# Chained copies and later transposes in layer 1, row sums ahead of widened reciprocals in layer 0, small loads by GpSimd at the head

## The chip, the core and the metric

The kernel runs on one core of a Trainium2 chip. A core has five engines that work side by side, each with its own in-order queue of instructions: TensorE (PE in the profile) multiplies matrices and writes the results to PSUM; VectorE (DVE) and ScalarE (ACT) compute on SBUF and PSUM; GpSimd (POOL) computes on SBUF; SyncE (SP) issues DMA transfers, which ACT and POOL can issue as well. Engines wait for each other by semaphores. The metric is the time of one execution on the device in microseconds, the median of several runs.

## What is computed

Eight images of 32 x 32 positions (1024 tokens) and 384 channels go through two layers. Layer 0 normalises by groups of channels and applies attention of six heads with 64 channels each, with learned tables of relative positions. Layer 1 applies causal attention of one head with 384 channels, and a feed-forward part with weights reduced to signs.

```python
# layer 0: attention over an image
qkv = gn(x) @ qkv_w + qkv_b                     # q, k, v of six heads
attn = (q * HD ** -0.5) @ k.T + rel_h + rel_w   # 1024 x 1024 for each head
x = x + softmax(attn) @ v @ proj_w + proj_b
# layer 1: attention over the same tokens, then the feed-forward part
q, k, v = (ln(t) @ w for w in (Wq, Wk, Wv))
t = t + softmax(causal(q @ k.T * C ** -0.5)) @ v
h = gelu(bitlinear(ln(t), W1, b1))
t = t + bitlinear(h, W2, b2)
```

The part `bitlinear` uses the signs of the weights' differences from group means and quantises its result by the largest absolute value of an image. Images 5, 6 and 7 get no feed-forward result.

## The kernel before

The images run one after the other in the order 5, 0, 1, 2, 3, 4, 6, 7 (`ORDER`), so "the first image" is image 5. The kernel is written in a framework that orders the instructions of each engine by priorities and a model of their times, allots buffers and sets all semaphores. The source steers this order with `tc.issue_after(ins)`: instructions inside such a block that run on the same engine as `ins` are placed behind it in that engine's queue. It adds no wait between engines. `behind_of` is the same, and does nothing when given none. PSUM has one pool of eight tiles of 128 x 512 (`o_tile`), one bank each; a tile is given out again once its readers are done.

**The head (`run`, L1366 on).** `load_factors` loads the two factors of layer 1's combined query-key weight by SP and ACT. `load_T` loads the first image transposed, in six pieces of 256 KB, three by SP and three by ACT. `load_weights` then issues the small loads by ACT: two for the rows of biases (L148, L149), four for the position table `rel` (L151, L152), whose rows are 252 bytes long; SP loads the weights (`wproj_sb`, three thirds of `qkv_w`, and two biases spread over the partitions). A square root on a constant (`early_root`) makes ACT load its table. PE multiplies the factors out (`multiply_out`, nine steps, f_wqk), in between forms the group means and variances (two small matmuls, f_gmean and f_gvar), turns the bias rows (`turn_biases`, L169) and adds the value bias times the projection to the projection bias (`join_biases`, L376, f_pb). ACT scales `rel` (L171) and copies and scales the biases (L170, L172, L173). DVE takes the statistics (L434), finishes the normalisation (L451, three slices of 1024 columns) and forms `fold` (L235), a small matrix of ones by which PE can add row sums. The first projection of queries (`project_qk`, f_qk at L558) needs the normalised image. POOL builds sums of weights (`weight_forms`). A matmul of fp32 data appears in the profile as two records.

**Product sets (`ProductSet`).** A product of 3 x 3 blocks of weights with 3 x 2 blocks of input is done with 15 multiplications in place of 18 (`PROD_ORDER`). Sums of inputs (`sum_forms`, L568) and of weights are made beforehand. Each product goes to one of six banks A to F; `keep` copies partial sums from a bank with ACT (L623), and `run` combines some copies (L643; on POOL in layer 1). When a bank has all its products and its partner is ready, `finish` calls `final`, which on DVE adds bank and copy into the result: `put_queries` (L1069) or `put_values` (L1077) in layer 1. `in_turn` gives all these matmuls one fixed order on PE.

**Layer 0's attention (`attend0_fast`).** Three pairs of heads times two halves of the queries, six stretches. In each, PE computes scores (L889, L893) for eight key tiles, ACT takes exponentials (L900), DVE adds the eight tiles up (`add_up`, L905, L907), and PE multiplies with the values (L915, f_av). The row sums follow: DVE transposes the total in 32 x 32 blocks (L924) and reduces it (`few`, L926). In five stretches `gathered` brings `few` into its layout by five DMAs and DVE adds (L952); in the last stretch PE adds by `fold` (L947, f_den). `reciprocals` takes the reciprocals (L954), records two checks (L545, L546), widens them by a copy (L958) and a block transposition (L959), and a multiplication scales the result oT. It is done one stretch later: for the fifth stretch (third pair, half 0) within the last one, and multiplied by DVE (L977); for the last stretch at once (L987). Then PE projects the result, eight tiles f_pj in three steps each (L504); the third step of tiles 0 to 3 reads what L977 wrote.

**Layer 1's head (`attention1`, L1086 on).** The projected tiles are added to the image (`more`, L995), normalised by rows in two halves of four tiles (`normed`: L461, L462, L465, ACT's root L467, the reciprocal L469 and four scalings L474, f_xn), and turned by PE (`turn_normed`, L414, f_pt, copied by ACT at L415). Half 0's query products run (`of_q`, f_pr_1q), in whose course half 1 is normalised and turned, followed by half 0's value products (`of_v`, f_pr_1v) and half 1's.

Of the kernel before, what the change touches and what calls it, by code (L numbers as in the profile page):

```python
# [11 lines left out]
F32 = mybir.dt.float32  # L12
# [79 lines left out]
def conv_attn_hybrid(  # L92
# [51 lines left out]
    def load_weights(pools):  # L144

        nc.vector.memset(rel, 0.0)
        rows = pools.page("rows")[: 3 * NC + NM, :P]
        nc.scalar.dma_start(out=rows[: 3 * NC, :], in_=qkv_b.rearrange("(m p) -> m p", p=P))  # L148
        nc.scalar.dma_start(out=rows[3 * NC :, :], in_=b1.rearrange("(m p) -> m p", p=P))  # L149
        for half in range(2):  # L150
            nc.scalar.dma_start(out=rel[half * HD : (half + 1) * HD, 0, : 2 * H - 1], in_=rel_hT)  # L151
            nc.scalar.dma_start(out=rel[half * HD : (half + 1) * HD, 1, : 2 * W - 1], in_=rel_wT)  # L152
# [8 lines left out]
        nc.sync.dma_start(out=b2_sb, in_=b2.partition_broadcast(P))  # L161

        early = pools.small.tile([P, 1], F32, tag="early", name="early_root")
        first_root[0] = nc.scalar.activation(early, ones[:, 0:1], AF.Sqrt).ins
        return raw, rows

    def turn_biases(pools, rows):
        ps = pools.o_tile("biases")
        nc.tensor.transpose(ps[:, : 3 * NC + NM], rows, ident[: 3 * NC + NM, : 3 * NC + NM])  # L169
        nc.scalar.copy(biases, ps[:, : 3 * NC + NM])  # L170
        nc.scalar.mul(rel, rel, 1.0 / qscale)  # L171
        nc.scalar.mul(bqk[:, 0:NPAIR], bqk[:, 0:NPAIR], qscale)  # L172
        nc.scalar.mul(bqk_neg, bqk, -1.0)  # L173
# [199 lines left out]
    def join_biases(pools):  # L373
        ps = pools.o_tile("pb")
        for k in range(NC):
            nc.tensor.matmul(  # L376
                ps[:, :C], bv[:, k : k + 1].to_broadcast([P, P]), wproj_sb[:, k, :], start=(k == 0), stop=(k == NC - 1)
            )
# [3 lines left out]
    def load_factors(pools):  # L382
# [4 lines left out]
        return wqT_sb, wkT_sb  # L387

# [16 lines left out]
    def stages(pools):  # L405

        last_transpose, last_mean, last_root, last_normed = [None], [None], [None], [None]

# [18 lines left out]
        def group_norm_T(b, xT=None):  # L427

            xT = load_T(b) if xT is None else xT
# [20 lines left out]
            for k in range(NC):  # L450
                nc.vector.tensor_scalar(  # L451
                    xT[:, k, :], xT[:, k, :], cs[:, 0:1], cs[:, 1:2], ALU.subtract, ALU.mult
                )
# [138 lines left out]
        class ProductSet:  # L592

            def __init__(self, name, forms, weights, width=512, tiles=None, bias=False, eng=None):
# [4 lines left out]
                self.full, self.behind = [], None  # L599
# [18 lines left out]
            def keep(self, ps, name):  # L618
                dst = self.kept(name)
                end = next((end for end in PROD_ENDS.values() if end[0] == name), None)  # L620
                with behind_of(self.behind):
# [251 lines left out]
        def attend0_fast(residual, b, q, k, r, v, later):  # L873
# [5 lines left out]
            last_exp, last_matmul = [None], [None]  # L879
# [41 lines left out]
            def over_tiles(p, half, total):  # L921
# [4 lines left out]
                nc.vector.tensor_reduce(few, tr.rearrange("p (a n i) -> p a n i", a=2, i=32), AX.X, ALU.add)  # L926
# [567 lines left out]
```

## Time and profile before

| | us |
|---|---|
| runs shown: lowest, median, highest of 3 | 2284.01, 2284.54, 2287.18 |
| the profiled execution | 2285.15 |
| its span, first to last instruction | 2283.4 |
| busy: ACT | 1208.8 (53%) |
| busy: POOL | 523.9 (23%) |
| chain that ended last: share of PE, DVE, DMA | 91%, 5%, 1% |
| granted TensorE clock | 0.998 |

An engine's busy time is the sum of its instructions. The waits list who stood idle, what ended it, the total, how often, and the longest. In a timeline each line has a start, a duration, the engine, the line of the source, the operation, the tile written and the tiles read, and how many instructions are merged; in brackets stands the idle time just before and what ended it. PE's ends are modelled and matmuls overlap in the pipeline, so that distances between starts say more than durations there. One image takes some 307 us; the first one's layer 0 projection starts at 164.89, the third one's at 710.48.

### The profile page before, as it was taken

The page shows a single profiled execution, that of the slowest core. Times are in us where ns is not written, and L with a number is a line of the kernel's source. Part 1 is how long each engine was busy: PE and PEld are TensorE (multiplying, and loading weights), DVE is VectorE, ACT ScalarE, POOL GpSimd, SP SyncE. Part 2 cuts the span into 40 slices and gives each one's busy share as a digit, 9 for nine tenths or more (in the row PEclk, how much of TensorE's full clock was granted, in tenths as well). Part 3 has the DMA queues.
Part 4 walks back from the last instruction along what each step waited for, and adds up shares of the span by engine and source line. Part 5 has one row for each costly group of instructions (what it writes and reads, how often), then busy time and mean ns, then how long its engine had stood idle before and what let it go on. Part 6 is the DMA issues. An engine that isn't in the chain of part 4 may idle for free.

```text
span 2283.4 us, 30117 instructions
## 1 busy us (share of the span) xinstructions
PE 2254.1 (99%) x10579; PEld 1382.8 (61%) x10579; DVE 1635.1 (72%) x2743; ACT 1208.8 (53%) x2181; POOL 523.9 (23%) x690
## 2 busy tenths in 40 slices
PE   8999999999999999999999999999999999999998
PEld 4547554768645677547685465874577754755474
DVE  6898578876888548886468884579854788737871
ACT  4654266337664457644467543766444766326641
POOL 6512222230141301313102313013040131221320
PEclk9999999999999999999999999999999999999999
DMA  7530562140730205520319203064002362017100
GB/s 182 155 92 28 157 140 59 39 165 29 150 103 29 73 39 125 127 58 1 111 43 184 55 29 111 28 147 106 30 20 92 96 147 68 1 52 160 43 1 30
DMA packets 182938, 188.54 MB, mean 83 GB/s; under 512 B 139717, under 2 KB 152378, under 8 KB 179962
## 3 DMA queue, kind: packets, MB, share of 16 engines
q1 hardware_dynamic: 164400, 115.85, 21.0%
q0 software_dynamic: 17184, 69.22, 9.7%
q8 instruction: 86, 1.41, 0.3%
q10 hardware_dynamic: 1194, 1.45, 0.2%
q14 instruction: 74, 0.61, 0.1%
HBM read 84.55 MB, written 51.58 MB: 60 GB/s over the span
## 4 chain that ended last, share of the span: by engine, by line
PE 91%; DVE 5%; DMA 1%; issue 1%; ACT 1%; ACTq 0%; DVEq 0%; SPq 0%
PE f_s L889 12%; PE f_av L915 12%; PE f_s L1157 8%; PE f_av L1172 8%; PE f_y L1332 7%; PE f_y L1282 7%; PE f_pj L504 5%; PE f_qk L558 5%; PE f_pr_A L558 4%; PE f_s L893 3%; PE f_pr_B L558 3%; DVE f_sum L907 3%; PE f_rel L558 2%; PE f_pr_1v_A L558 2%; PE f_pr_1q_A L558 2%; PE f_pr_1v_B L558 2%
## 5 line engine op out<-in xcount | busy, mean ns | idle before, releaser
L900 ACT ACTIVATE f_pr<-f_s 128x512 f32<-128x512 f32 x768 | 412.9, 595 | 41.7 <-PE f_s L893 37.9
L889 PE MATMUL f_s<-f_q,f_k 64*128 64x512 f32 x1536 | 398.9, 595 | 0.0
L907 DVE TENSOR_TENSOR f_sum<-f_sum,f_pr 128x1024 f32<-128x1024 f32 x288 | 374.4, 1300 | 26.4 <-DVE den L952 0.6
L915 PE MATMUL f_av<-f_pr,f_v 128*64 128x512 f32 x1536 | 340.2, 595 | 0.0
L893 PE MATMUL f_s<-f_r,unit 64*128 64x512 f32 x768 | 307.8, 793 | 0.0
L915 PEld LDWEIGHTS f_av<-f_pr,f_v 128*64 128x64 f32 x1536 | 106.0, 137 | 218.8 <-issue 191.9
L889 PEld LDWEIGHTS f_s<-f_q,f_k 64*128 64x128 f32 x1536 | 145.6, 186 | 124.3 <-issue 65.5
L1157 PE MATMUL f_s<-f_q,f_lnT 128*128 128x512 f32 (+3 forms) x576 | 198.2, 488 | 0.0
L1172 PE MATMUL f_av<-f_v,f_pr 128*128 128x385 f32 x576 | 195.3, 486 | 0.0
L780 POOL DMA_DIRECT2D f_r<-f_far x192 | 102.1, 534 | 392.6 <-DVE f_far L774 184.9
L1166 ACT ACTIVATE f_pr<-f_s 128x512 f32<-128x512 f32 (+3 forms) x96 | 47.0, 490 | 204.6 <-DVE f_s L1162 161.7
L1172 PEld LDWEIGHTS f_av<-f_v,f_pr 128*128 128x128 f32 x576 | 108.2, 190 | 77.3 <-issue 11.5
L1157 PEld LDWEIGHTS f_s<-f_q,f_lnT 128*128 128x128 f32 x576 | 100.8, 190 | 70.3 <-issue 46.9
L1293 DVE TENSOR_REDUCE am<-f_h 128x1 f32<-128x1024 f32 (+2 forms) x80 | 71.6, 946 | 95.6 <-ACT f_h L1286 95.6
L1286 ACT ACTIVATE f_h<-f_y,biases 128x256 f32<-128x256 f32 x240 | 100.7, 471 | 67.0 <-PE f_y L1282 67.0
L893 PEld LDWEIGHTS f_s<-f_r,unit 64*128 64x128 f32 x768 | 75.0, 187 | 89.9 <-issue 89.4
L558 PE MATMUL f_qk<-f_gnT,wq_sb 128*128 128x512 f32 x288 | 127.8, 595 | 0.0
L504 PE MATMUL f_pj<-wproj_sb,f_oT 128*128 128x384 f32 x384 | 127.3, 488 | 0.0
L1332 PE MATMUL f_y<-f_w2a,f_hilo 128*128 128x384 f32 x640 | 127.3, 341 | 0.0
L980 ACT COPY f_oT<-f_av 128x512 f32<-128x512 f32 x40 | 23.4, 585 | 190.1 <-PE f_av L915 190.1
L1332 PEld LDWEIGHTS f_y<-f_w2a,f_hilo 128*128 128x128 f32 x640 | 112.6, 188 | 3.8 <-issue 1.4
L905 DVE TENSOR_TENSOR f_sum<-f_pr,f_pr 128x1024 f32<-128x1024 f32 x48 | 62.4, 1299 | 72.5 <-ACT f_pr L900 72.5
(275 smaller groups left out, 4050.8 us busy)
## 6 DMA issues: line engine op xcount, KB each, us to landing
f_far<-f_far SPq DMA_DIRECT2D x48, 512.0 KB, 5.9
f_r<-f_far SPq DMA_DIRECT2D x192, 128.0 KB, 2.8
f_r<-f_far POOLq DMA_DIRECT2D x192, 128.0 KB, 4.4
f_far<-f_far SPq DMA_DIRECT2D x192, 64.0 KB, 4.7
f_x<-in_x SPq DMA_DIRECT2D x32, 384.0 KB, 3.8
f_gnT<-in_xT SPq DMA_DIRECT2D x21, 512.0 KB, 4.8
f_w1a<-w1s POOLq DMA_DIRECT2D x5, 1536.0 KB, 6.7
f_w2a<-w2s POOLq DMA_DIRECT2D x5, 1536.0 KB, 8.6
```

What stands on the lines that cost most here:

```text
L504: nc.tensor.matmul(ps[:, :C], xT[:, k, ts(j, P)], w[:, k, cols], start=(k == 0), stop=(k == NC - 1))
L558: last_product[0] = nc.tensor.matmul(*args, **kw).ins
L780: put = (nc.gpsimd if i else nc.sync).dma_start(out=r(part, p).bitcast(F32).rearrange("(m i) t -> i m t", i=4)[2 * i + d], in_=pages[i][ts ...
L889: nc.tensor.matmul(sc[par], k[rows[par], p, ts(c, P)], q[rows[par], p, ts(half, 512)], start=True, stop=False)
L893: last_matmul[0] = nc.tensor.matmul(sc[par], unit[rows[par], c // 2 % 2].rearrange("i h w -> i (h w)"), r(2 * (c // 4) + c % 2, p)[rows[pa ...
L900: last_exp[0] = nc.scalar.activation(pr[:, ts(par, 512)], sc[par], AF.Exp).ins
L907: adds.append(nc.vector.tensor_tensor(total, total, pr, ALU.add).ins)
L915: last_matmul[0] = nc.tensor.matmul(av[ts(par, HD), :], v[:, c, ts(2 * p + par, HD)], pr[:, ts(par, 512)], start=(c == 0), stop=(c == NJ - 1),
L1157: last_score[0] = nc.tensor.matmul(sc[:, lo:], xT[:, c // 4, k, ts(c % 4, P)], q[:, half, k, lo:], start=(k == 0), stop=(k == NC - 1),).ins
L1172: nc.tensor.matmul(av[:, : C + 1], prs[c][:, ts(j - c, P)], v[:, c, :], start=(c == 0), stop=(c == j))
L1282: nc.tensor.matmul(ps, w1k[i // 2][:, ts(m, P)], xs[i % 2][:, half, i // 2, :], start=(i == 0), stop=(i == 2 * NC - 1))
L1332: nc.tensor.matmul(ps[:, :C], h, w, start=(i == 0), stop=(i == len(products) - 1))
```

## The change

It has four parts.

- Layer 1: `keep` places each copy of a product set behind the set's previous copy on ACT. Of half 0's query products nine run with stores allowed, in whose course one store (bank D) can happen, and the tenth without; half 1's scaled tiles come behind that on DVE. The first value product and the last query product now run ahead of the transposes of half 1.
- Layer 0's attention: `reciprocals` is cut in two. In the last stretch, for the fifth one's sums, the reciprocal and its checks stay where they were, and the widening (now `widened`) and the multiplication come behind `few` on DVE. In the first image the fifth stretch's row sums are added by PE as well (`at_once`), without the five DMAs.
- The head: the loads of bias rows and position table are issued by POOL, ahead of the image's load in the source (`load_rows`). Three matmuls of 512 columns on zeros run first (`keep_busy`). The early root comes before the weights' loads. The bias rows are turned after six of nine factor steps; the three steps of the join are spread around the second mean; scaling of biases and of `rel` stand in `scale_biases` behind the second root, `rel` last.
- The first image's last normalisation step goes in two halves of 512 columns; the join's addition on DVE and `fold` come behind it.

```diff
@@ -143,13 +143,8 @@
-        nc.vector.memset(rel, 0.0)
-        rows = pools.page("rows")[: 3 * NC + NM, :P]
-        nc.scalar.dma_start(out=rows[: 3 * NC, :], in_=qkv_b.rearrange("(m p) -> m p", p=P))
-        nc.scalar.dma_start(out=rows[3 * NC :, :], in_=b1.rearrange("(m p) -> m p", p=P))
-        for half in range(2):
-            nc.scalar.dma_start(out=rel[half * HD : (half + 1) * HD, 0, : 2 * H - 1], in_=rel_hT)
-            nc.scalar.dma_start(out=rel[half * HD : (half + 1) * HD, 1, : 2 * W - 1], in_=rel_wT)
+        early = pools.small.tile([P, 1], F32, tag="early", name="early_root")
+        first_root[0] = nc.scalar.activation(early, ones[:, 0:1], AF.Sqrt).ins
         nc.sync.dma_start(out=wproj_sb, in_=proj_w.rearrange("(k p) o -> p k o", p=P))
@@ -159,18 +154,29 @@
         nc.sync.dma_start(out=b2_sb, in_=b2.partition_broadcast(P))
-
-        early = pools.small.tile([P, 1], F32, tag="early", name="early_root")
-        first_root[0] = nc.scalar.activation(early, ones[:, 0:1], AF.Sqrt).ins
-        return raw, rows
+        return raw
+
+    def load_rows(pools):
+        rows = pools.page("rows")[: 3 * NC + NM, :P]
+        nc.gpsimd.dma_start(out=rows[: 3 * NC, :], in_=qkv_b.rearrange("(m p) -> m p", p=P))
+        nc.gpsimd.dma_start(out=rows[3 * NC :, :], in_=b1.rearrange("(m p) -> m p", p=P))
+        nc.vector.memset(rel, 0.0)
+        for half in range(2):
+            nc.gpsimd.dma_start(out=rel[half * HD : (half + 1) * HD, 0, : 2 * H - 1], in_=rel_hT)
+            nc.gpsimd.dma_start(out=rel[half * HD : (half + 1) * HD, 1, : 2 * W - 1], in_=rel_wT)
+        return rows
...
         ps = pools.o_tile("biases")
-        nc.tensor.transpose(ps[:, : 3 * NC + NM], rows, ident[: 3 * NC + NM, : 3 * NC + NM])
+        turned = nc.tensor.transpose(ps[:, : 3 * NC + NM], rows, ident[: 3 * NC + NM, : 3 * NC + NM])
         nc.scalar.copy(biases, ps[:, : 3 * NC + NM])
-        nc.scalar.mul(rel, rel, 1.0 / qscale)
+        return turned.ins
+
+    def scale_biases():
         nc.scalar.mul(bqk[:, 0:NPAIR], bqk[:, 0:NPAIR], qscale)
-        nc.scalar.mul(bqk_neg, bqk, -1.0)
+        scaled = nc.scalar.mul(bqk_neg, bqk, -1.0).ins
+        with tc.issue_after(scaled):
+            nc.scalar.mul(rel, rel, 1.0 / qscale)
@@ -373,9 +379,9 @@
         for k in range(NC):
-            nc.tensor.matmul(
+            yield nc.tensor.matmul(
                 ps[:, :C], bv[:, k : k + 1].to_broadcast([P, P]), wproj_sb[:, k, :], start=(k == 0), stop=(k == NC - 1)
-            )
+            ).ins
         nc.vector.tensor_tensor(pb, pb, ps[:, :C], ALU.add)
@@ -385,6 +391,12 @@
         return wqT_sb, wkT_sb
+
+    def keep_busy(pools):
+        zeros, ps = pools.page("zeros"), pools.o_tile("zeros")
+        nc.vector.memset(zeros[:, :512], 0.0)
+        for n in (512, 512, 512):
+            nc.tensor.matmul(ps[:, :n], zeros[:, :P], zeros[:, :n], start=True, stop=True)
@@ -405,6 +417,7 @@
         last_transpose, last_mean, last_root, last_normed = [None], [None], [None], [None]
+        last_scaled = [None]
@@ -426,6 +439,7 @@
+            parts = 1 if xT is None else 2
             xT = load_T(b) if xT is None else xT
@@ -447,10 +461,12 @@
             nc.vector.reciprocal(cs[:, 1:2], d[:, 0:1])
-            for k in range(NC):
-                nc.vector.tensor_scalar(
-                    xT[:, k, :], xT[:, k, :], cs[:, 0:1], cs[:, 1:2], ALU.subtract, ALU.mult
-                )
+            for part in range(parts):
+                t = ts(part, T // parts)
+                for k in range(NC):
+                    last_scaled[0] = nc.vector.tensor_scalar(
+                        xT[:, k, t], xT[:, k, t], cs[:, 0:1], cs[:, 1:2], ALU.subtract, ALU.mult
+                    ).ins
@@ -596,7 +612,7 @@
                 self.left = {bank: sum(bank == o[0] for o in PROD_ORDER) for bank in "ABCDEF"}
-                self.full, self.behind = [], None
+                self.full, self.behind, self.last_copy = [], None, None
@@ -618,7 +634,7 @@
                 end = next((end for end in PROD_ENDS.values() if end[0] == name), None)
-                with behind_of(self.behind):
+                with behind_of(self.behind), behind_of(self.last_copy):
                     if not self.bias or end is None:
@@ -876,7 +892,7 @@
             rows = (slice(0, HD), slice(HD, P))
-            last_exp, last_matmul = [None], [None]
+            last_exp, last_matmul, last_few = [None], [None], [None]
@@ -923,7 +939,9 @@
                 few = pools.small.tile([P, 2, 16], F32, tag="few", bufs=2, name=f"few_{b}_{p}_{half}")
-                nc.vector.tensor_reduce(few, tr.rearrange("p (a n i) -> p a n i", a=2, i=32), AX.X, ALU.add)
+                last_few[0] = nc.vector.tensor_reduce(
+                    few, tr.rearrange("p (a n i) -> p a n i", a=2, i=32), AX.X, ALU.add
+                ).ins
                 return few
@@ -953,6 +971,9 @@
                 check(den, rt, b * PER_IMAGE + 2 * p + half)
+                return rt
+
+            def widened(p, half, rt):
                 room = pools.page(f"wide0_{b}_{p}_{half}")
@@ -973,8 +994,10 @@
                     with tc.issue_after(adds[4 if last else 5]):
-                        rb = reciprocals(*waiting)
-                    (nc.vector if last else nc.gpsimd).tensor_tensor(oT[:, p0, t0], oT[:, p0, t0], rb, ALU.mult)
+                        rt = reciprocals(*waiting)
+                    if not last:
+                        rb = widened(p0, waiting[1], rt)
+                        nc.gpsimd.tensor_tensor(oT[:, p0, t0], oT[:, p0, t0], rb, ALU.mult)
                 av = values(p, half, prs)
@@ -983,8 +1006,14 @@
                 few = over_tiles(p, half, total)
-                waiting = (p, half, few, None if last else gathered(p, half, few))
-            nc.vector.tensor_tensor(oT[:, p, t], av, reciprocals(*waiting), ALU.mult)
+                at_once = last or (b == ORDER[0] and p == NPAIR - 1)
+                if last:
+                    with tc.issue_after(last_few[0]):
+                        rb = widened(p0, waiting[1], rt)
+                    nc.vector.tensor_tensor(oT[:, p0, t0], oT[:, p0, t0], rb, ALU.mult)
+                waiting = (p, half, few, None if at_once else gathered(p, half, few))
+            rb = widened(p, half, reciprocals(*waiting))
+            nc.vector.tensor_tensor(oT[:, p, t], av, rb, ALU.mult)
             with behind_last():
@@ -1107,19 +1136,22 @@
                 of_q, of_v = products(0, forms)
-                of_q.run(10)
+                of_q.run(9, put_queries(0))
+                of_q.final = None
+                of_q.run(1)
                 with behind_of(last_ended[0]), behind_of(of_q.last_copy):
...
                 of_q.run(4, put_queries(0))
+                of_v.run(1)
+                of_q.run(1)
                 with behind_of(last_product[0]):
...
                 last_product[0] = last_transpose[0]
-                of_q.run(1)
                 forms = forms_of(1)
                 of_v0, (of_q, of_v) = of_v, products(1, forms)
-                of_v0.run(14, put_values(0))
+                of_v0.run(13, put_values(0))
                 of_q.run(1)
@@ -1365,29 +1397,39 @@
             factors = load_factors(pools) if pools.fast else None
+            if pools.fast:
+                keep_busy(pools)
+                rows = load_rows(pools)
             gn = load_T(ORDER[0], pools.fast)
             if pools.fast:
-                raw, rows = load_weights(pools)
+                raw = load_weights(pools)
                 plain.append(raw[0])
...
                 norm = group_norm_T(ORDER[0], gn)
+                next(norm)
                 for step in itertools.islice(factor, 2 * NC):
                     pass
-                next(norm)
+                with tc.issue_after(step):
+                    step = turn_biases(pools, rows)
+                with tc.issue_after(step):
+                    for step in itertools.islice(factor, 2):
+                        pass
                 with tc.issue_after(step):
                     next(norm)
-                for i in range(2):
-                    with tc.issue_after(last_mean[0]):
-                        step = next(factor)
-                with tc.issue_after(step):
-                    next(norm, None)
+                join = join_biases(pools)
                 with tc.issue_after(last_mean[0]):
...
                         pass
-                with tc.issue_after(step), tc.issue_after(last_root[0]):
-                    turn_biases(pools, rows)
-                    join_biases(pools)
+                with tc.issue_after(step):
+                    step = next(join)
+                with tc.issue_after(step):
+                    next(norm, None)
+                with tc.issue_after(last_root[0]):
+                    scale_biases()
+                with tc.issue_after(last_mean[0]):
+                    for step in itertools.islice(join, 2):
+                        pass
             else:
@@ -1400,7 +1442,9 @@
                     layer1_forms(pools, raw1[0], 0)
-                make_fold()
+                with tc.issue_after(last_scaled[0]):
+                    next(join, None)
+                    make_fold()
             for b in ORDER:
```

## The prediction

> **What bounds the kernel now.** I read the page's busy shares first, then the waits of TensorE, then timelines around each wait. TensorE (PE) is busy 99% of the span, VectorE (DVE) 72%, so only idle time of PE can be won, and PE's waits say where it is:
>
> ```profile
> PE 2254.1 (99%) x10579; PEld 1382.8 (61%) x10579; DVE 1635.1 (72%) x2743; ACT 1208.8 (53%) x2181; POOL 523.9 (23%) x690
> ...
> PE f_pt L414 <- DVE f_q L1069: 7.8, 8, 1.0
> PE f_wqk L395 <- DMA f_wqkT<-in_wkT: 6.3, 1, 6.3
> PE f_den L947 <- DVE few L926: 2.7, 8, 1.5
> PE f_bad L281 <- DVE worst L279: 1.9, 1, 1.9
> PE f_pb L376 <- ACT biases L170: 1.0, 1, 1.0
> ```
>
> Two of the five recur in each of the eight images (f_pt, f_den), two stand at the head (f_wqk, f_pb). The change touches all but f_bad. One image, the third in order, by engine:
>
> ```profile
> 710.25 0.29 PE L947 MATMUL f_den<-few,fold 128*64 128x16 f32 x4 [0.17 <-DVE few L926]
> 733.42 0.86 PE L414 MATMUL f_pt<-ident,f_xn 128*128 128x128 f32 x6
> 735.25 0.88 PE L414 MATMUL f_pt<-ident,f_xn 128*128 128x128 f32 x6 [0.97 <-DVE f_q L1069]
> 735.97 0.60 PE L558 MATMUL f_pr_1q_A<-f_xf,w1f 128*128 128x256 f32 x2
> 736.40 0.61 PE L558 MATMUL f_pr_1v_A<-w1f,f_xf 128*128 128x128 f32 x4
> ...
> 708.42 0.67 DVE L959 STREAM_TRANSPOSE f_wide<-f_wide 128x512 f32<-128x512 f32 x1
> 709.02 1.18 DVE L926 TENSOR_REDUCE few<-f_tr 128x32 f32<-128x1024 f32 x1
> 732.61 2.25 DVE L474 TENSOR_SCALAR f_xn<-f_x,lmv,lrs 128x384 f32<-128x384 f32 x4
> 734.78 0.41 DVE L1069 TENSOR_TENSOR f_q<-f_pr_1q_D,f_u_1q 128x256 f32<-128x256 f32 x1
> ```
>
> Two of four normalised tiles are turned at 733.42, then PE stands until 735.25. Six transposes take 0.72 of start to start (735.25 to 735.97), so PE was free at 734.14: 1.11 us lost. What ends the wait is not a tile but the first store of queries, f_q from bank D. The head:
>
> ```profile
> 6.34 6.57 PE L395 MATMUL f_wqk<-f_wqkT 128*128 128x384 f32 x12 [6.34 <-DMA f_wqkT<-in_wkT]
> 16.47 2.20 PE L376 MATMUL f_pb<-wproj_sb,biases 128*128 128x384 f32 x6 [1.02 <-ACT biases L170]
> ...
> 15.67 0.31 ACT L171 ACTIVATE rel<-rel 128x128 f32<-128x128 f32 x1 [0.69 <-DMA rel<-in_rel_wT]
> ```
>
> ACT stands in front of the rel table's DMA; the copy of the biases (16.25) is queued behind it, PE's join matmuls behind that, and the first projection f_qk follows only at 18.51, though the normalisation's first slice was done by about 16.0.
>
> [...] six product banks A to F and two transposed tiles fill them, so the third tile waits for D to be read. [...] Here the 12 first matmuls start 0.64 apart and turn to 0.32 at 10.98, that is 4.6 us after PE began. [...] The rel rows are 252 B; a DMA from GpSimd in this trace lands 4.4 us after issue (f_r).
>
> **Part 1, layer 1.** (a) A query store, D, is allowed within the first nine products, so it stands on DVE before the reciprocal of the second half's normalisation. It needs POOL's second subtraction, which ends at 731.77 (730.18 + 1.59); it would run from 731.85 to 732.26 (0.41). The reciprocal starts at 732.40 in any case, waiting for ACT's root: the store is free, hidden by that wait, and would cost its 0.41 if the root came earlier. POOL's subtraction is now waited for with the reciprocal, four scalings, five stores and eleven form sums behind it; the cushion is 0.14.
> (b) One value product and the last query product move ahead of the transposes: 0.43 (735.97 to 736.40) and 0.45 (four matmuls of 128 columns, 0.446 each in this stage) of PE work into the hole. Transposes then start at 733.42 + 0.88 = 734.30. The value product holds the seventh bank, tile 0 the eighth, tile 1 takes D (free from 732.3), tile 2 at 735.02 wants E. E's store comes right after the scalings, where D's stood: 735.19, PE at 735.25 as before. So the transposes end at 735.97 as before, and the 0.88 is simply gone; 0.23 of waiting is left. Bounds for one image: 0.45, if a tile must wait for F or for ACT's copy of tile 0; 1.11, if nothing waits. Take 0.88, times eight: **7.0** (3.6 to 8.9).
> What is late next: DVE's forms of the second half start 0.33 to 0.5 earlier, since one store is gone from that row; the query product C needs a bank at 743.96 - 0.88 = 743.08, and the value store that frees it ends at 743.26 - 0.45 = 742.8. Just enough. (c) Chaining a set's ACT copies costs nothing: in the windows I read they already run in that order.
>
> **Part 2, last half of layer 0.** The widening copy and its 32x32 transposition (0.33 + 0.60 start to start) leave the stretch before "few" and go behind it. "few" ends 0.9 earlier. PE loses little there: 32 f_av matmuls take 7.02 in the chain of waits, and in the second image 395.33 + 7.02 = 402.35 against the sum's start at 402.61: 0.26 for each of seven images, all removed. New behind it: the multiplication of half 0 of the third pair ended after few + 0.6, now after few + 0.35 + 0.71 + 0.7. In the third image that is 709.38 + 1.8 = 711.2; the projection's third slice wants it 1.30 after the sums, 709.95 + 1.30 = 711.25. A tie; a reciprocal slipped in between (0.17) makes PE stand. I take 0.1 for this (0 to 0.4), net 0.16 times seven = 1.1. First image: 164.66 - 156.12 - 7.02 = 1.52 lost. "few" comes 0.93 + 0.19 earlier (the gathered sum becomes a PE sum), that PE sum costs 0.29, and the multiplication is late by some 0.5: net 0.5. Together **1.6** (-1.5 to 3.3). The total of DVE's work is unchanged, so the later additions are not late.
>
> **Part 3, the head.** Small loads go from ACT's queue to POOL's, which is idle from 3.4: six issues at 0.53 end by about 7, and land by 11. POOL's first other work begins only at 16.5, waiting for weights, so nothing there is delayed. SP's weights no longer share semaphores with them and can be issued earlier[...]. The root's table load (1.28) leaves the stretch at 11.72. Three zero matmuls of 512 columns, six records at cold 0.85, fill PE from about 1.5 to 6.6; factors then run at 0.32 and end early. DVE loses the fold sum between statistics and aggregate (-0.16), the rel rows compete with the image's load (63 KB at 390 GB/s is 0.16[...]). Then, with PE free: aggregate ends 12.2, first mean at 12.6, one factor and one join step (four records, 1.3), second mean at 14.0 against 14.26, root, reciprocal, scaling from 15.0 against 15.20. Two joins (1.3) run beside it; the scaling in halves gives k = 0 by 15.4, k = 1 by 15.8, k = 2 by 16.2, and f_qk takes 0.86 for each. So f_qk starts near 15.5 against 18.51: 3.0. I take **2.8** (1.5 if the image lands over 1 us later, 3.4 if not at all). The join's addition and the fold (0.56 + 2 x 0.3) move behind the scaling on DVE, ahead of or among the 11 form sums, which end at 27.6; the next DVE work then comes at about 27.9, and forms are needed at 35. POOL's weight forms have the same start and 14 us to spare before their first use in the value products.
>
> **Sum.** 7.0 + 1.6 + 2.8 = 11.4. The profiled execution took 2285.15 (span 2283.4, 1.75 around it): 2273.75. The median is 0.6 below that execution: 2284.54 - 11.4 = **2273.1**.
>
> **Rivals.** Differences within 0.2% (4.6 us) can't be told from none here.
> A, the sum above: 70%, 2267.5 to 2279.
> B, the waits move on instead of going: tile 2 waits for ACT's copy, the late multiplication takes back part 2, bank C falls short. Only the head and some 0.2 an image are left: 2.8 + 1.6 = 4.4, 2280.1. For it: every cushion named is 0 to 0.3 us. Against: DVE has idle gaps of 0.4 to 0.6 before three f_pj additions, and 2.6 at 744.9, where it catches up. 14%, half of it within 0.2%.
> C, all cushions hold: 8.9 + 3.3 + 3.4 = 15.6, 2268.9. 9%.
> D, slower: the D store, queued on DVE ahead of the reciprocal, waits for POOL. If it came after POOL's third subtraction and its idle gap instead of its second (1.59 + 0.73 = 2.3 later), the scalings and transposes slip by 2.3 against 0.88 won: -1.4 an image, -11.4 in all, with 4.4 from the rest: 2291.5. It decides from a slip of 1.4 an image on (even), and 2.0 for 0.2%. For it: the cushion of 0.14. Against: POOL's subtraction ends where DVE idles, and POOL has gaps of 0.57 between them. 7%.
>
> The range takes A and C and most of B's faster part: 2267.5 to 2279.5. Faster: 70 + 9 + 6 = 85%; within: 8%; slower: 7%.
>
> **What will show it.** In each image's two groups of transposes, a distance near 0.95 instead of 1.83 (735.25 - 733.42), and the two products ahead of them; no PE wait on "few" but in the first image; f_qk from near 15.5, f_wqk at 0.32 from its first matmul. Wrong if DVE's reciprocal L469 waits for POOL, if f_pj's third slice waits for f_oT, or if the image's last load lands after 11.

## The result and the profile after

The kernel after takes 2274.53 us (median of 6 runs, 2274.21 to 2275.04), the kernel before beside it 2284.16: a ratio of 0.9956, 95% interval 0.9943 to 0.9969. The forecast was 2273.1 with 2267.5 to 2279.5. The profiled execution of after took 2274.38, its span is 2272.6.

Of the page's busy times, PE's and DVE's:

```profile
PE 2258.0 (99%) x10589; PEld 1384.9 (61%) x10589; DVE 1627.1 (72%) x2746; ACT 1208.3 (53%) x2181; POOL 527.9 (23%) x696
```

PE has ten records more than before (six on zeros, four for one more row sum of the first image) and is busy 3.9 longer; the time came out of its idle stretches. Of PE's waits in after (total, times, longest):

```profile
PE f_pj L520 <- DVE f_oT L1013: 1.4, 8, 0.2
```

The wait of f_pt on f_q (7.8) and the wait of f_den on few (2.7) are gone from the list; f_wqk and f_pb are gone from the head. New is a wait that comes eight times: the projection f_pj stands before a multiplication of DVE. It is one of the signs by which the prediction said that it would be wrong. The head, PE alone:

```profile
1.53 5.32 PE L399 MATMUL f_zeros<-f_zeros 128*128 128x512 f32 x6 [1.53 <-DVE f_zeros L397]
6.68 4.03 PE L407 MATMUL f_wqk<-f_wqkT 128*128 128x384 f32 x12
...
15.63 4.96 PE L574 MATMUL f_qk<-f_gnT,wq_sb 128*128 128x512 f32 x11
```

The first projection starts at 15.63 in place of 18.51. Layer 1 of the third image, all engines:

```profile
726.59 0.42 DVE L1098 TENSOR_TENSOR f_q<-f_pr_1q_D,f_u_1q 128x256 f32<-128x256 f32 x1
...
727.16 0.18 DVE L485 RECIPROCAL lrs<-lsd 128x4 f32<-128x4 f32 x1
...
727.38 2.24 DVE L490 TENSOR_SCALAR f_xn<-f_x,lmv,lrs 128x384 f32<-128x384 f32 x4
...
729.06 1.83 PE L427 MATMUL f_pt<-ident,f_xn 128*128 128x128 f32 x12
729.54 0.41 DVE L1098 TENSOR_TENSOR f_q<-f_pr_1q_E,f_u_1q 128x256 f32<-128x256 f32 x1
...
730.01 0.64 PEld L427 LDWEIGHTS f_pt<-ident,f_xn 128*128 128x128 f32 x6 [0.37 <-DVE f_q L1098]
```

Bank D's store now runs ahead of the reciprocal, which shows no wait in brackets. The twelve transposes stand on one line, 1.83 long, where before two groups of six began 1.83 apart; only the weight load of the third tile still waits, for bank E's store. It starts 0.95 behind the first tile (730.01 - 729.06), as forecast. The end of layer 0 in the same image:

```profile
704.06 0.42 DVE L979 COPY f_wide<-rt 128x512 f32<-128x512 f32 x1
...
704.92 0.26 DVE L972 RECIPROCAL rt<-f_den 128x16 f32<-128x16 f32 x1 [0.44 <-PE f_den L965]
705.09 0.65 DVE L980 STREAM_TRANSPOSE f_wide<-f_wide 128x512 f32<-128x512 f32 x1
...
705.78 0.69 DVE L1013 TENSOR_TENSOR f_oT<-f_oT,f_wide 128x512 f32<-128x512 f32 x1
...
706.53 4.78 PE L520 MATMUL f_pj<-wproj_sb,f_oT 128*128 128x384 f32 x14 [0.17 <-DVE f_oT L1013]
```

Here the change gives back what it wins. The last stretch's own reciprocal (704.92) stands between the widening copy and its transposition, and it waits 0.44 for PE's row sum. By starts on PE, the row sum follows the last f_av after 0.42 instead of 0.77 in images two to eight, and the projection's first step follows it after 0.60 instead of 1.00. But the third step follows the first after 1.73 instead of 1.39, and since its two records then stand 0.43 apart and not 0.32, the step behind it comes after 2.48 instead of 2.04. So 0.40 is won and 0.44 lost; the loss comes in all eight images.

### The profile page after: what moved, and what is told of

It reads as the page before. It is cut to its first block, busy times and chain, and to the rows that moved or that the text cites. A ratio compares the mean times of both kernels' runs of the same rounds, so it can differ in the third digit from the quotient of the medians.

```text
span 2272.6 us, 30133 instructions
## 1 busy us (share of the span) xinstructions
PE 2258.0 (99%) x10589; PEld 1384.9 (61%) x10589; DVE 1627.1 (72%) x2746; ACT 1208.3 (53%) x2181; POOL 527.9 (23%) x696
## 4 chain that ended last, share of the span: by engine, by line
PE 98%; DVE 1%; issue 0%; DVEq 0%
PE f_s L905 15%; PE f_av L931 15%; PE f_s L1189 8%; PE f_av L1204 8%; PE f_y L1364 7%; PE f_y L1314 7%; PE f_qk L574 6%; PE f_pj L520 5%; PE f_s L909 4%; PE f_pr_A L574 4%; PE f_pr_B L574 3%; PE f_rel L574 2%; PE f_pr_1v_A L574 2%; PE f_pr_1q_A L574 2%; PE f_pr_1v_B L574 2%; PE f_pr_1q_B L574 1%
## 5 line engine op out<-in xcount | busy, mean ns | idle before, releaser
L923 DVE TENSOR_TENSOR f_sum<-f_sum,f_pr 128x1024 f32<-128x1024 f32 x288 | 365.3, 1268 | 25.8
```

The lines of the kernel that those rows point to most:

```text
L923: adds.append(nc.vector.tensor_tensor(total, total, pr, ALU.add).ins)
```

## The experiments

Ten kernels ran, each timed in five rounds beside the kernel before, whose median was 2284.37, 2284.15 and 2284.87 in the three batches. Since a total is a poor witness for a part, the table has two places from each trace as well: the start of f_qk, and the start of f_bad, PE's last matmul, called the end of the work here. What lies behind it, up to the end of the span, took 8.1 to 9.9 in these traces. Both places come from a single profiled execution of each kernel. Seven kernels with after's head (after, e1, e2, e4, e7, e8, e10) start f_qk between 15.42 and 15.90, so the distance from f_qk to the end of the work tells more of a part behind the head than the end alone. Before's profiled execution lies 1.0 above its median, e5's 0.7.

| kernel | median us (lowest to highest) | f_qk | end of the work |
|---|---|---|---|
| before | 2284.16 (2283.84 to 2287.18) | 18.51 | 2273.76 |
| after | 2274.53 (2274.21 to 2275.04) | 15.63 | 2263.91 |
| e1: layer 1 as before | 2281.33 (2280.80 to 2282.90) | 15.83 | 2270.76 |
| e2: widening as before | 2275.34 (2274.81 to 2276.15) | 15.90 | 2263.60 |
| e3: head as before | 2276.94 (2276.36 to 2277.74) | 18.35 | 2266.54 |
| e4: own reciprocal later | 2271.41 (2271.14 to 2271.64) | 15.78 | 2260.54 |
| e5: no zeros | 2277.31 (2275.05 to 2277.97) | 18.12 | 2267.45 |
| e6: small loads by ACT | 2275.52 (2275.18 to 2277.15) | 16.93 | 2264.85 |
| e7: stores D and E first | 2279.39 (2278.53 to 2279.88) | 15.59 | 2268.58 |
| e8: e4, store E between | 2269.67 (2269.27 to 2270.32) | 15.48 | 2258.91 |
| e9: before, fewer POOL additions | 2283.68 (2283.54 to 2284.10) | 18.30 | 2272.31 |
| e10: copies not chained | 2281.04 (2280.73 to 2281.49) | 15.42 | 2270.69 |

**e1, layer 1 as before.** From after:

```diff
-                of_q.run(9, put_queries(0))
-                of_q.final = None
-                of_q.run(1)
+                of_q.run(10)
...
-                of_v.run(1)
-                of_q.run(1)
                 with behind_of(last_product[0]):
                     turn_normed(xT, 1, tiles)
                 last_product[0] = last_transpose[0]
+                of_q.run(1)
...
-                of_v0.run(13, put_values(0))
+                of_v0.run(14, put_values(0))
```

> The changed kernel with layer 1's order of before (ten query products without stores, transposes ahead of the last query and the first value product); the chained copies, the widening and the head stay as changed. Theory (each part is worth what PE lost at its own place): the distance from the second to the third transposed tile goes back to 1.25 in each image and the kernel loses 8 x 0.82 less two images' 0.15 = 6.3: about 2280.8. Rival (the parts share one slack, so that DVE or POOL would have held PE up elsewhere): it loses 3 or less, about 2277.5, and a new wait of PE stands in the table.

PE's waits in e1:

```profile
PE f_pt L427 <- DVE f_q L1098: 7.8, 8, 1.0
```

The wait is back whole. The end of the work comes 6.85 later, and from f_qk on the work takes 6.64 longer: 0.83 an image, against 0.88 in the forecast. The total (6.8 more than after) is near the theory's, and the rival is out.

**e2, widening as before.**

```diff
-                        rt = reciprocals(*waiting)
-                    if not last:
-                        rb = widened(p0, waiting[1], rt)
-                        nc.gpsimd.tensor_tensor(oT[:, p0, t0], oT[:, p0, t0], rb, ALU.mult)
+                        rb = widened(p0, waiting[1], reciprocals(*waiting))
+                    (nc.vector if last else nc.gpsimd).tensor_tensor(oT[:, p0, t0], oT[:, p0, t0], rb, ALU.mult)
...
-                at_once = last or (b == ORDER[0] and p == NPAIR - 1)
-                if last:
-                    with tc.issue_after(last_few[0]):
-                        rb = widened(p0, waiting[1], rt)
-                    nc.vector.tensor_tensor(oT[:, p0, t0], oT[:, p0, t0], rb, ALU.mult)
+                at_once = last
```

> The changed kernel with the widening back ahead of few, and the first image's fifth row sums by DMA again; the rest as changed. Theory (in images 2 to 8 the wait for few only moved to the third projection step, 0.35 won and 0.38 lost; the first image alone won some 1.05): f_den waits again 0.77 after the last f_av in seven images and about 2 us in the first, f_pj's third step follows at 1.39 instead of 1.73, and the total is 0.8 longer: 2275.3. Rival (my forecast's sizes: 0.16 an image and 0.5 in the first): 2276.1. Rival of no effect: 2274.5.

The median met the theory, and the theory fell all the same. PE's waits in e2:

```profile
PE f_den L965 <- DVE few L942: 1.5, 8, 0.2
```

The row sum waits again, the f_pj wait is gone, and no single wait on few is longer than 0.2: the first image has a gap of 0.79 there, not some 2 us. The end of the work comes 0.31 earlier than in after, and 0.59 earlier counted from f_qk. What makes e2's execution longer is the stretch behind the work, 9.94 instead of 8.68 from f_bad to the end of the span. So part 2 as written is worth nothing or a little less, and the gap of before in the first image is gone without it.

**e3, head as before.** All head parts of the diff are undone: the small loads by ACT and ahead of the root, no zeros, the old order of factors, biases and join, one scaling of 1024 columns.

> The changed kernel with the head of before (small loads by ACT, no zero matmuls, join after the scaling); layer 1 and the widening stay as changed. Theory: f_qk starts near 18.5 again and all later work is 2.8 to 2.9 later: 2277.4. Rival (a later image would absorb the head's gain, because DMA or POOL sets the pace there): less than 1.5 lost, under 2276.

f_qk starts 2.72 later and the work ends 2.63 later, so the head's gain reaches the end almost whole. The total is 2.4 above after, nearer to the theory's 2.9 than to the rival's 1.5. Parts three and four of the change are undone together here; what the two halves of the normalisation are worth by themselves was not tried.

**e4, the last stretch's own reciprocal behind the multiplication.**

```diff
-                    nc.vector.tensor_tensor(oT[:, p0, t0], oT[:, p0, t0], rb, ALU.mult)
+                    multiplied = nc.vector.tensor_tensor(oT[:, p0, t0], oT[:, p0, t0], rb, ALU.mult).ins
                 waiting = (p, half, few, None if at_once else gathered(p, half, few))
-            rb = widened(p, half, reciprocals(*waiting))
+            with tc.issue_after(multiplied):
+                rb = widened(p, half, reciprocals(*waiting))
             nc.vector.tensor_tensor(oT[:, p, t], av, rb, ALU.mult)
```

> The changed kernel with one more order: the last stretch's own reciprocal, checks and widening stand behind the multiplication of half 0 on DVE. Theory (the reciprocal waits for PE's sum between the widening copy and its transposition, and so makes the multiplication 0.6 late for the third projection step): that step follows at 1.39 or less after the first again, PE's wait for f_oT is gone, 0.38 an image: 3.0 less than the changed kernel, 2271.5. Rival (DVE's later additions are what holds PE, so the wait comes back at the first transposes or the fifth tile): 2274.5, with a new PE wait.

The third image in e4, all engines:

```profile
703.80 0.71 DVE L980 STREAM_TRANSPOSE f_wide<-f_wide 128x512 f32<-128x512 f32 x1
...
704.09 7.36 PE L520 MATMUL f_pj<-wproj_sb,f_oT 128*128 128x384 f32 x22
...
704.55 0.69 DVE L1013 TENSOR_TENSOR f_oT<-f_oT,f_wide 128x512 f32<-128x512 f32 x1
705.16 0.25 DVE L972 RECIPROCAL rt<-f_den 128x16 f32<-128x16 f32 x1
```

The multiplication follows at once, the projection's matmuls stand on one line without a wait, and the third step is back at 1.39. The work ends 3.37 earlier, 3.53 counted from f_qk (0.44 an image), and the median is 3.1 lower. This shows both the cause of the lost part and what the part is worth when nothing slips in.

**e5, without the zeros.**

```diff
             if pools.fast:
-                keep_busy(pools)
                 rows = load_rows(pools)
```

> The kernel after without its three multiplications of zeros; the order of the head's other work stays. Theory [...]: without them f_wqk's matmuls start near 5.3 us at about 0.5 us apart, [...] the first f_qk starts near 17.4 instead of 15.63, and the total is 2276.0 to 2276.6. Rival (the head is bound by the image's loads and statistics, and the order alone gave the gain): f_qk within 0.5 of 15.63, total 2274.4 to 2275.0.

PE in e5:

```profile
6.53 7.00 PE L401 MATMUL f_wqk<-f_wqkT 128*128 128x384 f32 x12 [6.53 <-DMA f_wqkT<-in_wkT]
```

The twelve factor records take 7.00 instead of 4.03. As the theory had it, the wide spacing of PE's first records then falls on the factors, but its size was too small: f_qk is 2.49 late, not some 1.8, and the total lies 0.7 above the theory's interval. PE's first matmul waits until 6.53 for its DMA, where the theory had 5.3; the records then run 0.64 apart, not 0.5, and stand at the later 0.32 only 5.9 after the first. In after the wide spacing falls on the zeros (0.85, against 0.43 for 512 columns in f_qk), and the factors stand 0.32 apart from the first, at 6.68. The work ends 3.54 later, because the first image loses another 1.04 ahead of its row sum (1.46 instead of 0.42). There a DVE copy took 7.26 beside POOL's additions; such a hold is told under e9.

**e6, small loads by ACT.** The six loads of `load_rows` are issued by ACT, behind its slices of the image.

```diff
-        nc.gpsimd.dma_start(out=rows[: 3 * NC, :], in_=qkv_b.rearrange("(m p) -> m p", p=P))
+        nc.scalar.dma_start(out=rows[: 3 * NC, :], in_=qkv_b.rearrange("(m p) -> m p", p=P))
...
-                rows = load_rows(pools)
             gn = load_T(ORDER[0], pools.fast)
             if pools.fast:
+                rows = load_rows(pools)
```

> The kernel after with the six small loads issued by ScalarE behind its part of the image's slices, as before; the order of what follows, the zeros and all else stay. Theory (the issuing engine is worth little by itself, because the biases' transposition has been moved off the path to f_qk): first f_qk within 0.5 of 15.63, total 2274.4 to 2275.1. Rival (ScalarE's issues hold its square root and the scaled weight product): f_qk at 16.5 or later and total 2275.6 or more.

PE's waits in e6:

```profile
PE f_biases L171 <- DMA f_rows<-in_b: 1.8, 1, 1.8
```

Neither theory holds. f_qk starts at 16.93, 1.30 late, as late as the rival had it, but not by ACT's root: the transposition of the bias rows, now placed ahead of six factor records, waits 1.80 on PE for their DMA. With ACT's later issue that place costs PE this wait; POOL's earlier issue is worth 0.9 at the end of the work.

**e7, both stores ahead of the reciprocal.**

```diff
-                of_q.run(9, put_queries(0))
+                of_q.run(10, put_queries(0))
                 of_q.final = None
-                of_q.run(1)
```

> The kernel after with both query stores, of banks D and E, ahead of the reciprocal on VectorE. Bank E's store waits for GpSimd's third subtraction, which ends near 727.8 in the first image of that size, so the reciprocal goes from 727.16 to about 728.4. Theory (the order on VectorE now sets when the transpositions run): the scalings end 1.2 later, the transpositions end 0.5 to 0.8 later in each image, total 2278.5 to 2281. Rival (the third tile has waited for bank E's store anyway, so an earlier store pays for the later scaling): no image loses more than 0.2, total 2274 to 2276.

The third image in e7, which is 1.09 late by the two images before it:

```profile
728.18 0.72 POOL L659 TENSOR_TENSOR f_u_1q<-f_u_1q 128x256 f32<-128x256 f32 x1 [0.57 <-ACT f_u_1q L639]
728.94 0.42 DVE L1098 TENSOR_TENSOR f_q<-f_pr_1q_E,f_u_1q 128x256 f32<-128x256 f32 x1 [0.84 <-POOL f_u_1q L659]
729.28 0.17 DVE L485 RECIPROCAL lrs<-lsd 128x4 f32<-128x4 f32 x1
...
730.53 1.32 PE L427 MATMUL f_pt<-ident,f_xn 128*128 128x128 f32 x9 [0.23 <-DVE f_xn L490]
```

DVE stands 0.84 before the store, and the reciprocal starts 1.03 later than in after (729.28 - 1.09 - 727.16). The transposes end 0.61 later in each image, and the total is 4.86 higher: the place that rival D named is real, and a slip of 1.03 costs 0.61.

**e8, e4 with bank E's store between the second and the third scaling.** From e4:

```diff
-                    tiles, _ = next(norm)
-                    tiles = list(tiles)
+                    rest, _ = next(norm)
+                    tiles = [next(rest), next(rest)]
                 last_ended[0] = last_normed[0]
-                of_q.run(4, put_queries(0))
+                of_q.final = put_queries(0)
+                of_q.finish()
+                with behind_of(last_ended[0]):
+                    tiles += list(rest)
+                last_ended[0] = last_normed[0]
+                of_q.run(4)
```

> The kernel of e4_recip_behind with bank E's query store between the second and the third scaling on VectorE instead of behind all four. Theory (the wait left ahead of the third tile's transposition is for that store): the store goes from near 729.5 to near 728.5, the third tile follows the second without the wait, 0.2 to 0.35 less in each image, total 2268.6 to 2269.9. Rival (the fourth scaling, now 0.4 later, takes its place, or the query stores behind it delay the next banks): total 2271.0 to 2272.

The third image in e8:

```profile
727.20 1.67 PE L427 MATMUL f_pt<-ident,f_xn 128*128 128x128 f32 x12
```

The twelve transposes now take 1.39 from first start to last start instead of 1.56, 0.17 an image, a little under what was expected; the total of 2269.67 is in the theory's interval. This is the fastest version: ratio to before 0.9936 (0.9923 to 0.9950), 4.9 us below after.

**e9, before with fewer additions on POOL.** From the kernel before:

```diff
-                for j in range(NJ):
+                for j in range(0 if b == ORDER[0] else NJ):
                     nc.gpsimd.tensor_tensor(xt[:, j, :], xt[:, j, :], pb, ALU.add)
```

> The kernel before, but in the first image GpSimd's eight additions of the projection's bias to the image (L868) are left out, so that image lacks this bias; all else stays. Theory (in before one VectorE addition at 95.1 us took 9.12 instead of 1.23 because GpSimd ran its additions back to back beside it): without them no VectorE instruction there takes over 2.6 us, TensorE's gap ahead of the first image's row sum falls from 2.05 to 0.77, and the total is 2282.5 to 2283.3. Rival (the hold comes from the transfers at that time or from the first image's own chain of row sums): the gap stays near 2.05 and the total near 2284.2.

The reason for it, in before's DVE queue alone, and then POOL's in the timeline of the same stretch:

```profile
95.11 9.12 DVE L907 TENSOR_TENSOR f_sum<-f_sum,f_pr 128x1024 f32<-128x1024 f32 x1
```

```profile
94.68 0.75 POOL L320 DMA_DIRECT2D f_w<-in_w1T  x1 [6.04 <-DMA parts<-f_few]
95.45 7.69 POOL L868 TENSOR_TENSOR f_x<-f_x,pb 128x384 f32<-128x384 f32 x8
```

and the same stretch of e9:

```profile
89.61 6.54 DVE L907 TENSOR_TENSOR f_sum<-f_sum,f_pr 128x1024 f32<-128x1024 f32 x5
```

With POOL's additions left out, five of DVE's take 6.54 together (start to start 1.3 each), and PE's gap ahead of the first row sum falls from 2.05 to 0.78. The work ends 1.45 earlier. The total is 1.2 below that of before in the same batch, but 0.4 above the interval expected, and its ratio (0.9985 to 1.0002) reaches 1: the cause is shown, its size only for the execution traced. The scatter says why. The 13 runs of e9 lie between 2283.54 and 2284.10, the 30 of before beside it between 2283.44 and 2287.46. The lowest times agree, and the long ones are gone, so what the hold costs seems to differ from execution to execution, up to some 4 us by this scatter. That is an estimate, since only one execution of before was traced.

**e10, copies not chained.**

```diff
-                with behind_of(self.behind), behind_of(self.last_copy):
+                with behind_of(self.behind):
```

> The kernel after without the chain of ScalarE's partial-sum copies: a copy is no longer kept behind the one before it. ScalarE's order then has the first values' second copy from bank B ahead of those from C and A. Theory (the chain is needed once a value product is moved ahead): the copy from A comes some 1.2 later, TensorE's next product into A, at 732.90 in the third image, waits for it, 0.7 to 1.0 in each image, total 2280 to 2282.7. Rival (the prediction's view, chaining neither costs nor brings anything): total 2274.3 to 2274.8.

PE's waits, and then the third image's timeline:

```profile
PE f_pr_1v_A L574 <- ACT f_u_1v L639: 4.5, 8, 0.6
```

```profile
734.50 0.37 ACT L639 COPY f_u_1v<-f_pr_1v_B 128x256 f32<-128x256 f32 x1 [0.97 <-PE f_pr_1v_B L574]
734.77 0.38 ACT L639 COPY f_u_1v<-f_pr_1v_C 128x256 f32<-128x256 f32 x1
735.03 0.39 ACT L639 COPY f_u_1v<-f_pr_1v_A 128x256 f32<-128x256 f32 x1
...
735.47 0.71 PE L574 MATMUL f_pr_1v_A<-w1f,f_xf 128*128 128x128 f32 x4 [0.57 <-ACT f_u_1v L639]
```

ACT idles 0.97 for bank B's second product while C and A, finished long before, are not copied; PE's next product into A then waits for that copy. From the last transpose to the first scores it is 19.97 again instead of 19.14, and the total is 6.5 above after. Without the chain, part 1's gain is lost again one step later.

## Why the prediction was right, and where not

The forecast asked for 11.4 less; 9.6 came in the medians and 9.85 at the end of the work.

- **Part 1** was right in mechanism and nearly in size: 7.0 forecast, 6.64 measured by e1. The reciprocal does not wait for POOL, the two products are ahead of the transposes, and the third tile waits for E's store as named. The cushions held: in the third image query product C starts 0.43 behind the product before it, without a wait. Images two and three lose 0.16 elsewhere (19.30 instead of 19.14 from the last transpose to the first scores). There the last value product into bank B starts late, just behind ACT's copy of that bank (749.31 and 749.36 in the third image). This is not due to part 1: e1 has the same 0.16 with layer 1 as before (20.13 against 19.97), and e3 and e6, with part 1, do not have it.
- **Its item (c)** said that chaining the copies costs nothing. True, but the reason given, that they run in that order already, was read from before, where no value product ran ahead. e10 shows that with it the chain is a condition of the gain.
- **Part 2** is the step that failed: "A tie; a reciprocal slipped in between (0.17) makes PE stand. I take 0.1 for this (0 to 0.4)". It did slip in, and it waits for PE's row sum itself (0.44 on DVE). PE lost 0.44 an image by it, just above the bound. That takes the part from 1.1 to nothing in seven images. The case was seen; its value was taken without asking where the scheduler would put the reciprocal and what that one waits for. Nor was there a tie without it. The third step was put 1.30 behind the sums at 709.95, which fits the start of the sums (710.25 in before, 0.3 earlier); in before that step starts 1.62 behind their start and 1.3 behind their end. In e4 the multiplication ends at 705.24 and the third step starts at 705.49, with 0.25 to spare.
- **Part 2's first image**, 0.5, was put down to the wrong cause. The 2.05 of before was mostly one DVE addition held beside POOL's (e9), and e2 shows a gap of 0.79 without part 2. So 1.3 of what the first image gains between the two traces is not the work of part 2 but luck: after's traced execution had no such hold. Why it had none is open; in e5, which differs from after by the zeros alone, a DVE copy in the same stretch is held for 7.26.
- **Part 3** was right: f_qk at 15.63 against "near 15.5", 2.63 at the end against 2.8. The zeros carry most of it (e5: 2.49 of f_qk), the early issue the next share (e6: 1.30); they overlap, so they don't add.
- **Rival D's** place is real (e7), its price of -1.4 an image was too high: the store behind POOL's third subtraction delays the reciprocal by 1.03, not 2.3. Rival B's "the late multiplication takes back part 2" is what happened, alone and without B's other two.

The total stayed in the range because part 2 was the smallest term, not because it held. Between the two traces the 9.85 can be made up from places: 2.88 ahead of f_qk, 6.64 for part 1 (e1), -0.59 for part 2 (e2), 1.24 for the hold (before against e9, from f_qk on) and -0.32 for the two waits at bank B come to 9.85. Each is read from single executions, and the medians, whose difference is 9.6, may contain less of the hold. Why the stretch behind f_bad differs between traces wasn't tried and stays open, and with one trace of each kernel it is not known whether the kernel or the execution sets it; in e2 it was 1.3 longer than in after, four times what its edit did to the end of the work.

## What to carry to other kernels

When an instruction is moved behind a wait, look at what the scheduler can put between its pieces, and what that newcomer waits for in its turn: here a "tie" was lost to an instruction that waits for the same producer. Read a part's effect from the distance at its own place in every repetition, and only then from the total; e2's total agreed with a theory that its trace contradicts. When a product is moved ahead, look at the order of its readers on the other engine's queue as well: in e10 the wait returned one bank later. And look at the scatter of the runs, not only at their median; in e9 it told of a wait that comes and goes.

## What the runs showed of the hardware

**A DVE instruction held through a series of POOL's, in some executions.** e9 is told above. In e3 it hit a copy with one input, in the timeline of all engines:

```profile
96.95 7.70 POOL L872 TENSOR_TENSOR f_x<-f_x,pb 128x384 f32<-128x384 f32 x8
...
97.59 7.35 DVE L967 COPY f_wide<-rt 128x512 f32<-128x512 f32 x1
```

The copy takes 7.35 instead of 0.42 and ends at 104.94, just after POOL's eighth addition (104.65). In after the same copy gets through:

```profile
93.42 8.92 POOL L884 TENSOR_TENSOR f_x<-f_x,pb 128x384 f32<-128x384 f32 x8
...
94.13 0.59 DVE L979 COPY f_wide<-rt 128x512 f32<-128x512 f32 x1
```

So a DVE instruction can last until eight of POOL's in a row are done, as this copy and before's addition (9.12 instead of 1.23) do. It need not: the copy began 0.64 after the start of POOL's first addition in e3 and 0.71 in after, where POOL's second addition took 1.20 instead of some 1.0. What DVE waits for there, and what decides between the two cases, is not shown. In e5 the copy was held like in e3 (7.26). In e7 and e8 five additions of DVE take 10.56 and 10.77 together, where e9's take 6.54, beside the four additions that POOL runs before it waits for the image's DMA (3.86 and 3.87 together), and no wait of PE on few stands in their lists.

**The time until PE's records stand at their later spacing varies.** The first records of an execution stand at twice the later distance: in before 0.64 for 384 columns, from 7.14 to 10.98, and 0.32 from 11.45 on; in after 0.85 for the zeros' 512 columns, from 2.54 to 5.96, and 0.43 in f_qk. The granted clock reads 1.00 on both sides of the change (before 6.3 to 11.4 and 11.4 to 19; after 1.5 to 6.7 and 6.7 to 11), so it does not tell the two apart, and what does is not shown. From PE's first matmul to the first record at the later spacing it took 3.3 in e3 and 5.1 in before, which have the same head, and 5.2 in after, 3.5 in e6 and 5.9 in e5. (The prediction's 4.6 for before ends at the record in which the spacing begins to change; that one is 0.47 long.) That is a difference of up to 2.6 us between five traces, and no run shows where it comes from. A forecast should carry it as a range.
